# Weight fetches spread over the first pass: q and k in halves beside four batches, v and layer 2's weights behind the last batch

## The chip, the cores and the metric

The kernel runs on one core of a Trainium2 chip. A core has a matrix engine (TensorE, PE in the profile), three engines for elementwise work (VectorE or DVE, ScalarE or ACT, GpSimd or POOL) and a sequencer that here issues nearly all DMA transfers (SyncE, SP). Each engine works through its own list of instructions in order; semaphores hold an instruction until what it needs has been done. On-chip memory is SBUF (128 partitions) and PSUM (the matrix engine's accumulators). The metric is the device time of one execution in microseconds (us), the median of several runs.

## The reference, cut to what matters

The input x has 8 images of 512 channels and 32 x 32 = 1024 positions, in float32. Four layers follow each other; the change concerns the first two.

```
# layer 0: f, g, h are 64-channel products of x; f and g are batch-normalised over ALL 8 images
f = relu(batchnorm(Wf x));  g = relu(batchnorm(Wg x));  h = Wh x
attn = (f^T g) / largest_singular_value(f^T g)
x = Wv (attn applied to h) + x
# layer 1: group norm, then full attention over 1024 positions
n = groupnorm(x);  q = wq n + bq;  k = wk n + bk;  v = wv n + bv
x = x + wp (softmax(q^T k / sqrt(512)) applied to v) + bp
# layer 2: attention with 128 channels (W_w gives t, p, g; Z_w leads back), scaled, + x
# layer 3: sign(x + bias) times sign(W) with a scale, batch norm, + x, parametric relu
```

wq, wk, wv, wp and layer 3's W are 512 x 512, 1 MB each.

## The kernel before, in words

**The first pass.** Layer 0's batch norm needs the statistics of all 8 images before f and g can be used, so the kernel first reads every image once. The loop at line 1367 goes over the batches b = 0 to 7. `load_x` (line 136) fetches the 2 MB of a batch in four DMAs of 512 KB, one for each chunk of 128 channels (five for batch 0). The tile `xt` has two buffers, so the fetch of batch b waits until the matrix engine has read batch b-2 for the last time. For each batch the matrix engine makes f, g and (for b below 6) h, in 16 half-width matmuls per product, which the profile shows at line 1381; chunk by chunk for f, then for g, then for h. Two of them run side by side. Batches 6 and 7 stay in SBUF for the main part, which takes them first; the others are fetched again later.

**The weights of layer 1.** The scores need only wu = wq^T wk and the values only wo = wp wv, so the kernel multiplies the weights with each other first (`product`, line 1420). That needs q, k and v with the output channel on the partitions, while they lie in memory with the input channel there. `load_blocks` (line 1339) fetches such a matrix in 16 DMAs of 64 KB (q over four partition groups, r over four groups of rows; the issues carry line 1345), and `natural` (line 1350) turns it with four transposes of 32 x 32 blocks on VectorE (line 1355). Buffers are reused: turned q lies in w3's buffer, turned k in the buffer of q's blocks, turned v in that of k's blocks, and the matrix p (wp) later takes the buffer of v's blocks.

**Order of the fetches.** All of this goes through SP's single list, in the order of the loop: batch 1 and w3; batch 2 and all of q; batch 3 and all of k; batch 4, all of v and `load_rows` (11 small DMAs, lines 212 to 219); batch 5; batch 6 with z and tpg, the weights of layer 2 (line 156); batch 7; and p's four DMAs (line 1563), the first of them ahead of batch 7. The built program gives every DMA one of eight completion semaphores in turn, so each DMA issue also waits until the DMA eight places before it has landed.

**After the loop.** The matrix engine's order is written by hand from line 1581 on, with a generator `filler` (line 1556) that deals out work that depends on nothing urgent: the products for wu, the h of batches 6 and 7 (`late_h`), scaling of z, biases (`biases`, which reads turned k and p), Gram matrices, and last the products for wo (turned v times p). Between these pieces stands a chain of small steps, which normalises f and g (`relu`, line 1512), turns them (`turn`, line 1269), forms Gram matrices and finds the largest singular value by repeated squaring. The other engines' lists follow from the program's order and a scheduler that places each operation by its own estimate of when it can run.

**The main part** (from line 1645) then takes the 8 batches one after the other through all four layers; it is untouched.

Of the kernel before, what the change touches and what calls it, by code (L numbers as in the profile page):

```python
# [8 lines left out]
F32 = mybir.dt.float32  # L9
# [7 lines left out]
P = 128  # L17
# [53 lines left out]
QUAD = 32  # L71
GROUPS = 16
# [15 lines left out]
def kernel(  # L88
# [21 lines left out]
    wpool = ctx.enter_context(tc.tile_pool(name="weights", bufs=1))  # L110
# [8 lines left out]
    def wide():  # L119
        return psum["wide"].tile([P, N], F32, tag="wide", name="wide")  # L120
# [4 lines left out]
    def bank():  # L125
        return psum["bank"].tile([P, HF], F32, tag="bank", name="bank")
# [9 lines left out]
    def load_x(b, split=False):  # L136
        t = xpool.tile([P, CC, N], F32, tag="x", name="xt")
        src = x[b].rearrange("(cc p) n -> p cc n", p=P)
        for cc in range(CC):
            for ns in [half(h) for h in range(NH)] if split and not cc else [slice(0, N)]:  # L140
                nc.sync.dma_start(out=t[:, cc, ns], in_=src[:, cc, ns])
        return t

    def half(i):
        return bass.ts(i, HF)

    def side(i):

        return slice(i * MID, (i + 1) * MID)


    sbw = {}

    def load_w(name, src, shape, pool=wpool, eng=nc.sync, tag=None):
        t = pool.tile(shape, F32, tag=tag or name, name=name)
        eng.dma_start(out=t, in_=src)
        sbw[name] = t
        return t
# [4 lines left out]
    a1 = early.enter_context(tc.tile_pool(name="a1", bufs=1))  # L163
# [47 lines left out]
    def load_rows():  # L211
        nc.sync.dma_start(out=bg_row, in_=rows[MID + C :].partition_broadcast(P))
        rv = rows[MID : MID + C].rearrange("(q m b) -> q b m", q=4, b=QUAD)
        rq = cols.rearrange("(m b) n -> n b m", b=QUAD)
        for q in range(4):
            nc.sync.dma_start(out=bvc[bass.ts(q, QUAD), :], in_=rv[q])
            nc.sync.dma_start(out=bqc[bass.ts(q, QUAD), :], in_=rq[COL["L1_conv_bq"] + q])
        for i in range(2):
            nc.sync.dma_start(out=wv2[side(i), :], in_=w_v0)
# [58 lines left out]
    wu = wpool.tile([P, CC, C], F32, tag="wu", name="wu")  # L278
# [990 lines left out]
    def turn(b, src, dst, k):  # L1269

        tp = quad()
        for i in range(4):
            nc.tensor.transpose(tp[:, i, :], src[:, bass.ts(i, P)], ident)
        to = dst.rearrange("p (h t) c -> p h t c", t=4)[:, :, :, side(b % 2)]
        tp = tp.rearrange("p t (h c) -> p h t c", c=MID)
        if k:
            nc.scalar.copy(to, tp)
        else:
            nc.vector.tensor_copy(to, tp)

    def sign_weights():

        w3 = sbw["w3"]
        sign = a1.tile([P, CC, C], F16, tag="sign", name="sign")
        absw = a1.tile([P, 2, C], F32, tag="absw", name="absw")
        for cc in range(CC):
            nc.scalar.activation(sign[:, cc, :], w3[:, cc, :], AF.Sign)
            nc.scalar.activation(absw[:, min(cc, 1), :], w3[:, cc, :], AF.Abs)
            if cc:
                nc.vector.tensor_tensor(absw[:, 0, :], absw[:, 0, :], absw[:, 1, :], ALU.add)  # L1290
        lo, hi = sign[:, :, 0 : C // 2], sign[:, :, C // 2 :]
        nc.vector.scalar_tensor_tensor(sw3, hi, PACK, lo, ALU.mult, ALU.add)
        return absw[:, 0, :]
# [42 lines left out]

    nat = {}

    def load_blocks(name, src, tag):

        t = sbw[name] = a1.tile([P, 4, GROUPS, QUAD], F32, tag=tag, name="blocks_" + name)
        of = src.rearrange("(r a) c o -> r a c o", a=QUAD)
        for q in range(4):
            for r in range(4):
                nc.sync.dma_start(  # L1345
                    out=t[bass.ts(q, QUAD), r].rearrange("a (c m) b -> a c (m b)", c=CC),
                    in_=of[r][:, :, bass.ts(q, P)],
                )

    def natural(name, tag):  # L1350

        t = nat[name] = a1.tile([P, CC, C], F32, tag=tag, name="nat_" + name)
        to = t.rearrange("p o (c r a) -> p r c o a", r=4, a=QUAD)
        for r in range(4):
            nc.vector.transpose(to[:, r], sbw[name][:, r].rearrange("p (c o) b -> p c o b", o=CC))

    later = {
        1: [("w3", w_3, a1)],
        6: [("z", w_z, wpool), ("tpg", w_tpg, wpool)],
    }  # L1360
    shapes = {"z": [P, C], "tpg": [P, CC, 3 * P]}

# [4 lines left out]
    for b in range(B):  # L1367
        xt = load_x(b) if b else first
        for name, src, pool in later.get(b, ()):
            load_w(name, src, shapes.get(name, [P, CC, C]), pool)  # L1370
        if b in (2, 3, 4):
            load_blocks(*((("q", w_q, "q"), ("k", w_k, "k"), ("v", w_v, "v"))[b - 2]))
        if b == 4:
            load_rows()
        if b >= B - 2:
            resident[b] = xt
        banks = [bank() for _ in w0[: 3 if b < B - 2 else 2]]

        def products(i, cc):
            for h in range(NH):  # L1380
                mm(  # L1381
                    out=banks[i][side(h), :],
                    lhsT=w0[i][:, cc, :],
                    rhs=xt[:, cc, half(h)],
                    start=cc == 0,
                    stop=cc == CC - 1,
                )

        if b == 0:
            for cc in range(CC):  # L1390
                for i in range(2):
                    products(i, cc)
        for i in range(3):
            if i == 2 and b >= B - 2:
                continue
            if b or i == 2:
                for cc in range(CC):
                    products(i, cc)
            if i == 0:
                nc.scalar.copy(fs[b], banks[i])  # L1400
                nc.vector.bn_stats(st[:, 0, b, :], fs[b])
            elif i == 1:
                nc.vector.tensor_copy(gs[b], banks[i])
                nc.vector.bn_stats(st[:, 1, b, :], gs[b])
                if last is not None:
                    turn(last[0], last[1], ht_pair[last[0] // 2], 0)
        if b < B - 2:
            hraw = a2.tile([P, HF], F32, tag="hraw", name="hraw")
            nc.scalar.activation(hraw, banks[2], AF.Identity, bias=bhc)
            last = b, hraw  # L1410
        else:
            last = None
        if b == 3:
            total3 = sign_weights()
        if b == 5:
            scale_signs(total3)
        if b > 4:
            natural(*((("q", "w3"), ("k", "q"), ("v", "k"))[b - 5]))

    def product(lt, rhs, dst, vector):  # L1420
        for i in range(CC // 2):
            ps = wide()
            for k in range(2):
                for oc in range(CC):
                    one = mm(  # L1425
                        out=ps[:, half(k)],
                        lhsT=lt[:, oc, bass.ts(2 * i + k, P)],
                        rhs=rhs[:, oc, :],
                        start=oc == 0,
                        stop=oc == CC - 1,  # L1430
                    )
                    if i + k + oc == 0:
                        tc.keep_in_program_order(one)
                    if k == 0 or oc < CC - 1:
                        yield
            to = dst[:, 2 * i : 2 * i + 2, :].rearrange("p o c -> p (o c)")
            if i % 2 and vector:
                nc.vector.tensor_copy(to, ps)
            else:
                nc.scalar.copy(to, ps)  # L1440
            yield
# [114 lines left out]
    def filler():  # L1556

        t = sbw["p"] = a1.tile([P, CC, C], F32, tag="v", name="p")  # L1560
        of = w_p.rearrange("(m b) c o -> c b m o", b=QUAD)
        for q in range(4):
            nc.sync.dma_start(out=t[bass.ts(q, QUAD)], in_=of[q])
        yield from product(nat["q"], nat["k"], wu, True)
        for b in order[:2]:
            yield from late_h(b)
        yield from gram(jl, 2, ht_pair[jl], gtl)
        scale_z()
        yield
        between = biases()  # L1570
        sums = sums_u()
        for j in rest:
            for _ in grams(j):
                next(sums, None)
                yield
                if next(between, None):
                    yield
        yield from product(nat["v"], sbw["p"], wo, False)
# [251 lines left out]
```

## Time and profile before

| what | before |
|---|---|
| median of 3 runs (lowest to highest) | 1888.45 us (1888.18 to 1890.97) |
| time of the profiled execution | 1889.26 us |
| span in its profile, first to last instruction | 1887.4 us |
| matrix engine busy | 1855.8 us, 98% of the span |
| first pass, up to wu's first product | 0 to 103.83 us |
| hand-ordered stage after it, up to the main part's first product | 103.83 to 191.69 us |
| main part | 191.69 to 1887 us |
| DMA queue of SP: bytes over the span | 64.96 MB |

In the profile's lines a group is named by engine, line of the kernel, operation and tiles (out<-in); "x16" counts instructions; a bracket gives the idle time before the instruction and what ended it. PEld is the load of a matmul's stationary operand, which runs beside PE. SPq is SP's own time for issuing DMAs. PEclk is the clock that the matrix engine was granted, as a share of full speed.

### The profile page before, as it was taken

Reading aid. Unit: us, or ns where it says so; the run is one execution under the profiler, and the core shown is the slowest. Engines: PE = TensorE matmul, PEld = TensorE weight load, DVE = VectorE, ACT = ScalarE, POOL = GpSimd, SP = SyncE. Lnnn points to the kernel's source line nnn. Section 1 sums busy time; section 2 is a strip of 40 time slices with the busy share of each in tenths; the row PEclk is TensorE's granted clock in tenths of the full one; section 3 lists DMA queues with packets and bytes.
Section 4 is the critical chain, followed back from the end, with each engine's and each line's share of the span. In section 5 each row is a group of like instructions: output and inputs, shape, how many; then the busy total and the mean of one; then the engine's idle time right before and its main releaser. Section 6 shows DMA issues by size and latency. Waiting matters only on the chain.

```text
span 1887.4 us, 16534 instructions
## 1 busy us (share of the span) xinstructions
PE 1855.8 (98%) x6196; PEld 948.2 (50%) x6196; DVE 1121.6 (59%) x2083; ACT 542.0 (29%) x882; POOL 121.9 (6%) x109
## 2 busy tenths in 40 slices
PE   9799999999999999999999999999999999999997
PEld 4246455544645455544645455544645455544653
DVE  3246696467774666467764676357643766355447
ACT  2032221144203521244202522144202521244114
POOL 1000000100020000200020001100020001000011
PEclk9899999999999999999999999999999999999999
DMA  7720000002000110002000110001000200000001
GB/s 250 232 81 7 1 6 12 1 16 85 18 1 1 65 41 12 1 22 79 18 0 1 69 37 12 1 34 67 12 0 12 90 12 1 1 34 23 12 0 46
DMA packets 32738, 66.52 MB, mean 35 GB/s; under 512 B 4944, under 2 KB 12300, under 8 KB 32524
## 3 DMA queue, kind: packets, MB, share of 16 engines
q1 hardware_dynamic: 31724, 64.96, 10.3%
q8 instruction: 51, 0.84, 0.2%
q10 hardware_dynamic: 864, 0.43, 0.1%
q14 instruction: 35, 0.29, 0.0%
q0 software_dynamic: 64, 0.00, 0.0%
HBM read 46.44 MB, written 18.94 MB: 35 GB/s over the span
## 4 chain that ended last, share of the span: by engine, by line
PE 94%; DMA 2%; DVE 2%; SPq 1%; ACT 1%; issue 0%; POOL 0%; ACTq 0%; DVEq 0%
PE bank L412 46%; PE bank L590 20%; PE bank L992 6%; PE bank L839 6%; PE bank L691 3%; PE bank L708 3%; PE bank L1381 2%; DMA xt<-in_x 2%; PE bank L436 1%; PE bank L731 1%; PE wide L1425 1%; SPq L1345 1%; PE bank L1060 1%; PE bank L1483 1%; PE bank L862 0%
## 5 line engine op out<-in xcount | busy, mean ns | idle before, releaser
L590 PE MATMUL bank<-e,vt 128*128 128x512 f32 x768 | 336.2, 594 | 0.0
L590 PEld LDWEIGHTS bank<-e,vt 128*128 128x128 f32 x768 | 144.3, 190 | 172.3 <-issue 167.9
L412 PE MATMUL bank<-ut,h 128*128 128x512 f32 x384 | 178.9, 597 | 0.0
L412 PEld LDWEIGHTS bank<-ut,h 128*128 128x128 f32 x384 | 71.3, 190 | 94.7 <-issue 93.0
L412 PE MATMUL bank<-us,hs 128*128 128x512 f32 x256 | 115.6, 593 | 0.0
L839 PE MATMUL bank<-tpg 128*128 128x512 f32 x256 | 115.4, 595 | 0.0
L992 PE MATMUL bank<-e,tpg 128*128 128x512 f32 x256 | 114.7, 595 | 0.0
L363 DVE TENSOR_TENSOR e<-bank,e 128x512 f32<-128x512 f32 x96 | 66.1, 689 | 60.8 <-PE bank L412 42.4
L846 ACT ACTIVATE e<-bank 128x512 f32<-128x512 f32 x128 | 76.3, 597 | 67.0 <-PE bank L839 67.0
L412 PE MATMUL bank<-h,wu 128*128 128x512 f32 x192 | 89.0, 594 | 1.7 <-DVE h L487 1.7
L357 ACT COPY e<-bank 128x512 f32<-128x512 f32 x96 | 56.1, 585 | 118.9 <-PE bank L412 118.5
L412 PE MATMUL bank<-wo,h 128*128 128x256 f32 x384 | 89.9, 384 | 0.0
L243 POOL TENSOR_TENSOR r_r<-r_v,minus_half 128x4 f32<-128x4 f32 (+1 forms) x11 | 10.9, 989 | 1058.2 <-DVE r_v L242 1052.9
L1381 PE MATMUL bank<-xt,fg 128*64 128x512 f32 x256 | 63.7, 644 | 15.3 <-DMA xt<-in_x 10.7
L992 PEld LDWEIGHTS bank<-e,tpg 128*128 128x128 f32 x256 | 48.1, 190 | 60.4 <-issue 60.0
L412 PEld LDWEIGHTS bank<-wo,h 128*128 128x128 f32 x384 | 71.4, 190 | 12.6 <-issue 3.8
L412 PEld LDWEIGHTS bank<-us,hs 128*128 128x128 f32 x256 | 48.4, 190 | 57.5 <-issue 54.5
L851 DVE TENSOR_TENSOR esum<-esum,e 128x1024 f32<-128x1024 f32 x48 | 58.8, 1225 | 30.1 <-ACT e L846 29.9
L839 PEld LDWEIGHTS bank<-tpg 128*128 128x128 f32 x256 | 47.6, 190 | 55.0 <-issue 52.4
L719 ACT ACTIVATE sg<-xt,rb 128x512 f16<-128x512 f32 x64 | 44.2, 716 | 107.5 <-DVE xt L710 104.6
L363 DVE TENSOR_TENSOR vt<-bank,vt 128x512 f32<-128x512 f32 x48 | 33.2, 691 | 66.4 <-PE bank L412 65.6
L357 ACT COPY vt<-bank 128x512 f32<-128x512 f32 x64 | 37.3, 584 | 121.3 <-PE bank L412 121.2
(361 smaller groups left out, 2884.3 us busy)
## 6 DMA issues: line engine op xcount, KB each, us to landing
xt<-in_x SPq DMA_DIRECT2D x55, 512.0 KB
out<-both SPq DMA_DIRECT2D x63, 256.0 KB
rfull<-r_dram SPq DMA_DIRECT2D x15, 512.0 KB
f_dram<-f SPq DMA_DIRECT2D x8, 256.0 KB
fb<-f_dram SPq DMA_DIRECT2D x8, 256.0 KB
w<-in_w SPq DMA_DIRECT2D x1, 1024.0 KB
blocks_q<-in_w_q SPq DMA_DIRECT2D x16, 64.0 KB
blocks_k<-in_w_k SPq DMA_DIRECT2D x16, 64.0 KB
```

What stands on the lines that cost most here:

```text
L357: nc.scalar.copy(dst, ps)
L363: nc.vector.tensor_tensor(dst, ps, u, ALU.add)
L412: mm(out=ps[:, q * w : (q + 1) * w], lhsT=lt(ka, kb, q, k), rhs=rhs(ka, kb, q, k), start=first and q == 0 and k == 0, stop=last and k == 1 ...
L590: mm(out=ps, lhsT=a[:, t, bass.ts(r_, P)], rhs=e[t], start=first and t == 0, stop=last and t == NTH - 1, skip_group_check=True,)
L691: mm(out=ps[:, i, :], lhsT=xt[:, cc, bass.ts(4 * h + i, P)], rhs=sbw["tpg"][:, cc, 2 * P : 3 * P], start=cc == 0, stop=cc == CC - 1,)
L708: mm(out=ps, lhsT=sbw["z"][:, bass.ts(oc, P)], rhs=att, start=True, stop=True)
L719: nc.scalar.activation(sg[:, cc, :], xt[:, cc, half(h)], AF.Sign, bias=rb3[:, cc : cc + 1])
L839: mm(out=ps, lhsT=pt[:, 0, bass.ts(t, P)], rhs=tt[:, 0, half(h)], start=True, stop=True,)
L846: nc.scalar.activation(e[:, half(h)], ps, AF.Exp, scale=float(P) ** -0.5)
L851: nc.vector.tensor_tensor(esum, esum, e, ALU.add)
L992: mm(out=banks[h], lhsT=gt[:, t, :], rhs=es[t][:, half(h)], start=t == 0, stop=t == NT - 1,)
L1381: mm(out=banks[i][side(h), :], lhsT=w0[i][:, cc, :], rhs=xt[:, cc, half(h)], start=cc == 0, stop=cc == CC - 1,)
```

## The change

`load_blocks` takes the row groups r that it shall fetch, and keeps one tile per matrix over several calls. In the loop q's first half (r = 0, 1; 8 DMAs of 64 KB) is fetched beside batch 2, its second half beside batch 3, k's halves beside batches 4 and 5. z and tpg move from batch 6 to batch 7, and v's 16 DMAs come behind the loop. `natural` runs for q at b = 6 and for k at b = 7 (one batch later than before), and for v in `filler`, behind wu's products and ahead of the h of batches 6 and 7. The fetch of p moves behind it, for it reuses the buffer of v's blocks. No operation is added or removed, no shape or buffer changes.

```diff
-    def load_blocks(name, src, tag):
-        t = sbw[name] = a1.tile([P, 4, GROUPS, QUAD], F32, tag=tag, name="blocks_" + name)
+    def load_blocks(name, src, parts):
+        if name not in sbw:
+            sbw[name] = a1.tile([P, 4, GROUPS, QUAD], F32, tag=name, name="blocks_" + name)
+        t = sbw[name]
         of = src.rearrange("(r a) c o -> r a c o", a=QUAD)
         for q in range(4):
-            for r in range(4):
+            for r in parts:
                 nc.sync.dma_start(
...
     later = {
         1: [("w3", w_3, a1)],
-        6: [("z", w_z, wpool), ("tpg", w_tpg, wpool)],
+        7: [("z", w_z, wpool), ("tpg", w_tpg, wpool)],
     }
...
-        if b in (2, 3, 4):
-            load_blocks(*((("q", w_q, "q"), ("k", w_k, "k"), ("v", w_v, "v"))[b - 2]))
+        if b in (2, 3, 4, 5):
+            load_blocks(*((("q", w_q), ("k", w_k))[b // 2 - 1]), ((0, 1), (2, 3))[b % 2])
         if b == 4:
             load_rows()
...
-        if b > 4:
-            natural(*((("q", "w3"), ("k", "q"), ("v", "k"))[b - 5]))
+        if b > 5:
+            natural(*((("q", "w3"), ("k", "q"))[b - 6]))
+    load_blocks("v", w_v, range(4))
...
     def filler():
+        yield from product(nat["q"], nat["k"], wu, True)
+        natural("v", "k")
         t = sbw["p"] = a1.tile([P, CC, C], F32, tag="v", name="p")
         of = w_p.rearrange("(m b) c o -> c b m o", b=QUAD)
         for q in range(4):
             nc.sync.dma_start(out=t[bass.ts(q, QUAD)], in_=of[q])
-        yield from product(nat["q"], nat["k"], wu, True)
         for b in order[:2]:
             yield from late_h(b)
```

## The prediction, made before the changed kernel had run

> **What bounds the kernel now.** I read the page's slices first (40 slices of 47 us), then the windows of the three stages, since an average of 98% hides where the matrix engine stands still.
>
> ```profile
> PE   9799999999999999999999999999999999999997
> PEclk9899999999999999999999999999999999999999
> DMA  7720000002000110002000110001000200000001
> ...
> 0.00:103.83 103.83, 88.56 (x385) 34.27 (x385) 32.69 (x79) 14.47 (x23) 5.09 (x26) 0.95 0.73 230
> 103.83:191.69 87.86, 82.27 (x706) 50.34 (x705) 49.95 (x166) 30.88 (x60) 2.27 (x3) 1.00 0.10 34
> ```
>
> In the window lines the columns are length, busy PE, PEld, DVE, ACT, POOL, then granted clock, DMA share, GB/s. Only the first pass (to 103.83 us) is both short of matrix work (88.56 of 103.83 busy), slowed in clock (0.95), and full of DMA (0.73). Everything later is bound by the matrix engine with DMA nearly idle, and its order is relative: nothing there happens at a fixed time. So what the first pass gains or loses should appear in the end.
>
> Next the matrix engine's timeline around the hole, in microseconds from the start and duration:
>
> ```profile
> 38.93 7.09 PE L1381 MATMUL bank<-xt,fg 128*64 128x512 f32 x32
> 46.53 3.65 PE L1381 MATMUL bank<-xt,h 128*64 128x512 f32 x16
> 51.84 1.08 PE L1381 MATMUL bank<-xt,fg 128*64 128x512 f32 x4 [1.66 <-DMA xt<-in_x]
> 53.29 1.08 PE L1381 MATMUL bank<-xt,fg 128*64 128x512 f32 x4 [0.37 <-DMA xt<-in_x]
> 55.12 1.08 PE L1381 MATMUL bank<-xt,fg 128*64 128x512 f32 x4 [0.75 <-DMA xt<-in_x]
> 58.15 6.21 PE L1381 MATMUL bank<-xt,fg 128*64 128x512 f32 x20 [1.95 <-DMA xt<-in_x]
> 64.88 3.65 PE L1381 MATMUL bank<-xt,h 128*64 128x512 f32 x16
> 74.55 5.71 PE L1381 MATMUL bank<-xt,fg 128*64 128x512 f32 x14 [6.02 <-DMA xt<-in_x]
> ```
>
> Batch 3 runs without a hole; batches 4 and 5 wait for their x chunk by chunk, and run slowly behind each wait: in the window 74.5 to 84.1 the clock was 0.73. The size of the loss, from starts: batch 2 starts at 27.89 and batch 3 at 38.93, so a batch with h takes 11.04 us. From batch 3's start to the end of batch 7 (38.93 to 103.9) lie 65.0 us; unstalled they would be 3 x 11.04 (batches 3, 4, 5) + 1.0 (the eight small L1298 matmuls, 88.22 to 89.21) + 7.6 (batch 6, 89.21 to 96.81) + 7.09 (batch 7) = 48.8. The loss is **16.2 us**.
>
> Then why x is late, from the chain of waits between 40 and 76 us:
>
> ```profile
> 33.98 7.88 DMA xt<-in_x
> 41.88 0.56 SPq L1345
> ...
> 46.97 0.60 SPq L1345
> ...
> 47.67 0.53 SPq L141
> ...
> 49.37 8.73 DMA xt<-in_x
> 58.12 0.56 SPq L1345
> ...
> 69.70 0.60 SPq L219
> 70.39 4.02 DMA xt<-in_x
> ```
>
> SP issues in order, and a DMA waits for the one eight places before it. So of 16 blocks seven go out at once, the eighth waits until x has landed (41.88, 58.12), and it and eight more follow at 0.64 us each. Only then does SP reach the next batch's x, at 47.67 and, with 6.0 us of row loads besides, at 70.39. The buffer of xt had been free since about 39 and 50. SP's issue time bounds this, not bandwidth: between 41.9 and 47.6 the blocks move 9 x 64 KB in 5.7 us, about 100 GB/s, where x moved at about 410 GB/s after 76 us.
>
> **What the Trainium skill says.** "DMA: Bandwidth & Descriptors", Rules for kernel authors, says that transfers of less than 64 KB are mostly overhead; these, at the edge, agree with it: 0.64 us of SP each. The same page, Anatomy of one DMA: a semaphore wait is made by the issuing sequencer before dispatch, the DMA engines never wait. That is the stall above: one waiting block holds back all x behind it. "TensorE: Matmul & The Clock Gate", Part 1: after about 3.4 us idle the clock is halved until a busy window of like length; the trace agrees in kind, with 6.21 us for 20 matmuls after 58.15 (20/32 of 7.09 is 4.43). The same page, Architectural detail: VectorE's queue is strictly first in, first out. That matters for v.
>
> **The change part by part.**
>
> *The halves.* With 8 blocks beside batch 2 the eighth still waits for x2 at 26.66, but is then the last: SP is free at 27.3 instead of 32.4. Batch 3's x waits for its buffer (batch 1 ends at 24.41 + 3.65 = 28.06), goes out at 28.1 and, since in before it landed 9.4 us after its first issue beside seven blocks (32.47 to 41.88), lands at 37.5; the matrix engine wants it at 38.93. Batch 4: SP free at 38.1, buffer at 35.45 + 3.65 = 39.1, landed 9.4 to 10.4 us later (47.67 to 58.12 is the other example), at 48.5 to 49.5; wanted at 49.97. Both stalls are gone.
>
> *Batch 5.* Half of k's blocks and the row loads stand before it. Eighth block at 48.5 to 49.5, + 0.6, + 6.0 for the rows: x5 goes out at 55.1 to 56.1. Its chunks arrive, as batch 4's did in before (51.84, 53.29, 55.12, 58.15 against 47.67), 4.2, 5.6, 7.4 and 10.4 us later; without blocks beside them the last came after about 8.5 (a load at 78.84 against 70.39). Last chunk: 63.6 to 66.5. The matrix engine starts batch 5 at 61.0 and wants the last chunk 2.65 later, at 63.7. So 0 to 2.8 us of stall remain, and 0 to 1.8 of slow clock behind it (6.21 against 4.43 above). I take **2.5** of loss.
>
> *Batches 6 and 7.* The eighth block of k's second half waits for x5 (65.1), so x6 goes out at about 65.7 and lands 8.5 later, at 74.2; wanted at 61.0 + 11.04 + 1.0 + 2.5 = 75.6. Batch 7 goes out when batch 5 is read, about 74.6, first chunk 78.8; wanted at 83.2. No stall. Batch 7 ends at about 90.3 instead of 103.9.
>
> *z, tpg and v last.* They leave SP's path ahead of x and stand behind x7: 2 MB of x, 1 MB of z and tpg, and seven blocks at about 400 GB/s are 8.6 us, with start-up about 12, so tpg lands at 86.6; nine blocks at 0.64 follow, last issue 92.4, landed about 2.5 later (estimate from traffic of the last v block, 63.75 to about 65.9): **95**. The built order puts v's four transposes on VectorE between the turn copies ft and gt (at 113.6 in before, which is 9.7 us after batch 7's end) and the Gram copies. At 90.3 + 9.7 = 100 they find v landed, 5 us early. They cost 4 x 0.62 = 2.47 us (the row at 66.21), and VectorE stands idle there:
>
> ```profile
> 113.82 0.69 DVE L1279 COPY gt<-quad 128x512 f32<-128x512 f32 x1 [0.18 <-PE quad L1273]
> 116.76 0.22 DVE L1492 COPY gm<-bank 64x64 f32<-64x64 f32 x1 [2.25 <-PE bank L1483]
> 118.91 0.22 DVE L1492 COPY gg_full<-bank 64x64 f32<-64x64 f32 x1 [1.93 <-PE bank L1483]
> ```
>
> One transpose (0.62) stands ahead of gt in a gap of 0.18, so gt is 0.4 late; but the gt Gram waits for ScalarE's gt copy, which ends at 116.0, later anyway. Two fit into 2.25, one into 1.93. Cost 0; bound 2.5 if that cover is gone.
>
> *The rest at nothing.* q's and k's transposes fall on idle VectorE too (k's second half is due at about 69, landed at about 68 to 70, with the copy of g at batch 6 the next on the queue, some 10 us later). f's write-out behind v's blocks on SP: ready at about 98, SP free at 93. p now waits for v's transposes, goes out at about 104 and needs some 7 us; biases and wo use it from about 42 us after batch 7 (146 in before), 132. fb of batch 7 comes behind p; batch 7 enters only in the main part. Cover of tens of microseconds in each.
>
> *Sum.* 16.2 - 2.5 - 0 to 0.5 for v = 13.5 us. Profiled execution 1889.26 (1.9 over the span, 0.8 over the median) - 13.5 = 1875.8; against the median, **1875.0 us**.
>
> **The rivals.** (a) Batch 5's x comes in time: 16.2 gained, 1872.2. For it: 63.6 is the early end of its arrival; against it: seven blocks run beside it, and all x beside blocks took 9.4 to 10.4. (b) SP still starves the pass: x4 or x5 or x6 later than I think, each followed by a slow clock (batch 5 lost 6.02 + about 2.5 in before). Half of the gain goes: 8 us left, 1880.5. For it: the margin of batch 4 is 0.5 to 1.5 us on its first chunk and that of x6 1.4. (c) Slower: v is late for VectorE. The first transpose heads a strict queue, behind it stand gt and the Gram copies, and behind those the singular value chain and then the matrix engine. Every microsecond past 100 costs one; the kernel is slower only if v lands after 100 + 13.5 = 113.5, 18 us later than worked out; at 120 it would be 1895. Against it: tpg and 16 blocks would need twice their time. (d) No change: the next stage is bound by ScalarE's activations, say, so gains are given back. Against it: that stage starts from batch 7's last product, and all in it moves along. 1888.5.
>
> **How the numbers follow.** Likeliest, 12 to 15 us gained (1873.5 to 1876.5): 0.50. Rival (a), over 15: 0.22. Rival (b), between 4 and 12: 0.20. (d), within 0.2% (3.8 us, about what a measurement here can tell from no change): 0.04. (c) or another slowdown: 0.04. Faster is thus 0.92. The range runs from 16.9 gained (all stalls and a little of the first batches') to 7.5 gained, 1871.5 to 1881.0, which leaves out the tails of (b), (c) and (d).
>
> **What would show it.** In the profile after: no wait for xt at batches 3, 4, 6 and 7, up to 2.8 us at batch 5; batch 7 ending near 90; clock near 1 in that window; wu's products starting there; v's transposes running at about 100 without a wait for a DMA; the hand-ordered stage still 88 us, the main part 1695. I am wrong if VectorE waits for v's blocks, if SP reaches x5 much after 56, or if the stage after the pass grows by what the pass lost.

## The result, and the profile after

The changed kernel takes 1875.08 us in the median (1874.54 to 1875.96), beside 1888.62 us for the kernel before on the same chip: a ratio of 0.9926, with a 95% interval of 0.9909 to 0.9943. It is faster by 13.5 us. Two later comparisons of the same two kernels gave 0.9924 (0.9910 to 0.9937) and 0.9931 (0.9917 to 0.9944). The forecast was 1875.0 us. The profiled execution took 1875.41 us (1889.26 before), its span is 1873.6 us (1887.4).

The page's slices of the changed kernel, and its three stages as windows (length, busy PE, PEld, DVE, ACT, POOL, granted clock, DMA share, GB/s):

```profile
PE   9999999999999999999999999999999999999997
PEclk9999999999999999999999999999999999999999
DMA  8620000002000200002000200001000200000001
...
0.00:89.88 89.88, 83.46 (x384) 33.83 (x384) 30.36 (x75) 14.49 (x23) 5.09 (x26) 1.00 0.76 249
89.88:177.66 87.78, 82.28 (x707) 50.34 (x705) 52.21 (x170) 30.90 (x60) 2.27 (x3) 1.00 0.17 51
177.66:1873.00 1695.34, 1685.03 (x5108) 863.56 (x5108) 1039.09 (x1839) 496.98 (x799) 114.53 (x80) 1.00 0.07 23
```

The whole gain is in the first row: 103.83 us have become 89.88, and the clock of that stage 1.00 instead of 0.95. The second stage is as long as before (87.78 for 87.86) although VectorE does 2.3 us more there (v's transposes), and the main part is unchanged. Nothing was given back.

The matrix engine's timeline, batches 3 to 7 of the changed kernel:

```profile
38.50 7.04 PE L1383 MATMUL bank<-xt,fg 128*64 128x512 f32 x32
...
49.54 7.04 PE L1383 MATMUL bank<-xt,fg 128*64 128x512 f32 x32
...
60.58 1.89 PE L1383 MATMUL bank<-xt,fg 128*64 128x512 f32 x8
63.30 1.08 PE L1383 MATMUL bank<-xt,fg 128*64 128x512 f32 x4 [0.84 <-DMA xt<-in_x]
65.62 4.51 PE L1383 MATMUL bank<-xt,fg 128*64 128x512 f32 x20 [1.23 <-DMA xt<-in_x]
...
82.86 7.09 PE L1383 MATMUL bank<-xt,fg 128*64 128x512 f32 x32
89.88 2.84 PE L1428 MATMUL wide<-nat_k,nat_q 128*128 128x512 f32 x6
```

Batches 3, 4, 6 and 7 follow without a wait. Only batch 5 still waits, 2.1 us in two pieces; behind them 20 matmuls take 4.51 us, full speed, where they took 6.21 behind batch 4's waits in before. The chain of waits names what stood ahead of batch 5's x:

```profile
40.04 6.87 DMA xt<-in_x
46.92 0.56 SPq L1347
47.53 1.31 SPq L212
...
53.25 0.60 SPq L219
...
55.47 10.10 DMA xt<-in_x
65.62 4.51 PE bank L1383 x20
```

One block (line 1347) after batch 4's landing, then 6.4 us of row loads, then x. Nine blocks per batch had stood there before.

### The profile page after: what moved, and what is told of

Its sections match the earlier page's. It is cut to its first block, busy times and chain, and to the rows that moved or that the text cites. A ratio compares the mean times of both kernels' runs of the same rounds, so it can differ in the third digit from the quotient of the medians.

```text
span 1873.6 us, 16533 instructions
## 1 busy us (share of the span) xinstructions
PE 1850.8 (99%) x6196; PEld 947.7 (51%) x6196; DVE 1121.7 (60%) x2083; ACT 542.4 (29%) x882; POOL 121.9 (7%) x109
## 4 chain that ended last, share of the span: by engine, by line
PE 95%; DVE 2%; DMA 1%; ACT 1%; SPq 0%; issue 0%; POOL 0%; ACTq 0%; DVEq 0%
PE bank L412 46%; PE bank L590 21%; PE bank L992 6%; PE bank L839 6%; PE bank L691 3%; PE bank L708 3%; PE bank L1383 3%; PE bank L731 1%; PE bank L436 1%; DMA xt<-in_x 1%; PE wide L1428 1%; PE bank L1060 1%; PE bank L1486 1%; PE bank L862 0%; PE quad L1273 0%; DVE st L448 0%
## 5 line engine op out<-in xcount | busy, mean ns | idle before, releaser
L412 PEld LDWEIGHTS bank<-wo,h 128*128 128x128 f32 x384 | 71.4, 190 | 12.6 <-issue 3.8
L363 DVE TENSOR_TENSOR vt<-bank,vt 128x512 f32<-128x512 f32 x48 | 33.2, 691 | 66.4 <-PE bank L412 65.6
L357 ACT COPY ut<-bank 128x512 f32<-128x512 f32 x48 | 28.1, 586 | 128.7 <-PE bank L412 128.7
```

The costliest lines, as they stand in the source:

```text
L357: nc.scalar.copy(dst, ps)
L363: nc.vector.tensor_tensor(dst, ps, u, ALU.add)
L412: mm(out=ps[:, q * w : (q + 1) * w], lhsT=lt(ka, kb, q, k), rhs=rhs(ka, kb, q, k), start=first and q == 0 and k == 0, stop=last and k == 1 ...
```

## The experiments

Three measures help to compare them, all read from the matrix engine's timeline of one profiled execution. "First pass" runs from the first matmul to wu's first product; it leaves out the start, which varies by 0.6 us between profiles. "Batches 0, 1" runs from the first matmul to batch 2's first. "Lost at" a batch is what lies over 11.04 us between the h products of the batch before and its own; 11.04 is the spacing without a wait. All are in us.

| kernel | first pass | batches 0, 1 | lost at 4 | lost at 5 | hand-ordered stage | time, median |
|---|---|---|---|---|---|---|
| before | 99.30 | 23.4 | 7.3 | 8.7 | 87.86 | 1888.6 |
| changed | 85.53 | 23.1 | 0 | 2.5 | 87.78 | 1875.1 |
| changed, again | 83.54 | 23.6 | 0 | 0 | 87.76 | 1873.8 |
| changed, third time | 84.17 | 23.6 | 0 | 0.6 | 87.77 | 1874.4 |
| v alone last | 86.94 | 24.3 | 2.5 | 0.2 | 88.30 | 1876.8 |
| halves alone | 95.20 | 23.4 | 0 | 11.9 | 87.93 | 1885.2 |
| rows behind v | 83.28 | 23.3 | 0 | 0 | 87.77 | 1873.0 |
| k's second half at 6 | 83.44 | 23.5 | 0 | 0.1 | 87.76 | 1873.3 |
| both of these | 83.24 | 23.3 | 0 | 0.1 | 87.75 | 1873.4 |
| z, tpg at 6 | 88.94 | 24.2 | 0 | 4.8 | 87.76 | 1874.8 |
| blocks by GpSimd, free | 94.29 | 27.2 | 0 | 0 | 87.87 | 1884.4 |
| blocks by GpSimd, held back | 87.89 | 23.4 | 4.6 | 0 | 89.36 | 1880.6 |
| v fetched four times | 84.79 | 23.5 | 0 | 1.4 | 98.45 | 1885.0 |

Four profiles have no wait for x at all and take 83.24 to 83.54 us; what separates them lies mostly in batches 0 and 1, which took 23.1 to 24.3 us wherever the edit did not reach them. The floor is taken as 83.2 to 83.3, so before lost 16.0 us against it (16.2 was worked out). The kernel before took 1888.0 to 1888.6 us beside them, and the ratios ran from 0.9919 to 0.9986; those of the kernels within 1 us of the changed one have overlapping intervals.

**Which part brings it: v alone.** In the kernel before, v's fetch goes behind the loop, its transposes into the filler, p behind them; q and k stay whole.

```diff
-        if b in (2, 3, 4):
-            load_blocks(*((("q", w_q, "q"), ("k", w_k, "k"), ("v", w_v, "v"))[b - 2]))
+        if b in (2, 3):
+            load_blocks(*((("q", w_q, "q"), ("k", w_k, "k"))[b - 2]))
...
-        if b > 4:
-            natural(*((("q", "w3"), ("k", "q"), ("v", "k"))[b - 5]))
+        if b in (5, 6):
+            natural(*((("q", "w3"), ("k", "q"))[b - 5]))
+    load_blocks("v", w_v, "v")
...
```

> The kernel before with one part of the change alone: v fetched behind the loop, turned in the filler, p behind it; q and k whole beside batches 2 and 3. Theory (16 blocks beside batch 3 still hold batch 4's x, but nothing more than the row loads holds batch 5's): batch 4 loses 3.5 us of waiting and up to 1.8 of slow clock, batch 5 nothing; 11 to 12.7 of the 16.2 us are gained, batch 7 ends between 91 and 93, 1876.8 us. Rival (the halves are what counts, v last only takes 1 MB off): 3 to 5 us gained, 1884.

Measured: 1876.81 us, ratio 0.9939 (0.9922 to 0.9955). The pass is 3.7 us over the floor: 2.5 at batch 4, 0.2 at batch 5, and 1.0 in batches 0 and 1, which the edit does not touch. Batch 4:

```profile
47.30 3.65 PE L1381 MATMUL bank<-xt,h 128*64 128x512 f32 x16
51.37 1.08 PE L1381 MATMUL bank<-xt,fg 128*64 128x512 f32 x4 [0.41 <-DMA xt<-in_x]
52.61 1.08 PE L1381 MATMUL bank<-xt,fg 128*64 128x512 f32 x4 [0.16 <-DMA xt<-in_x]
54.27 1.08 PE L1381 MATMUL bank<-xt,fg 128*64 128x512 f32 x4 [0.59 <-DMA xt<-in_x]
55.83 4.51 PE L1381 MATMUL bank<-xt,fg 128*64 128x512 f32 x20 [0.48 <-DMA xt<-in_x]
```

Batch 4's x went out at 47.05, still behind 16 blocks of k; batch 5 no longer waits. This one part gives 12 of the 16 us.

More than batch 5's loss went: batch 4 lost 7.3 us in before and 2.5 here, though the same 16 blocks stand ahead of its x. Three things differ. Seven blocks of v no longer run beside it, and its last chunk came 8.7 us after it went out instead of 10.5. It went out 3.7 us ahead of the time at which batch 4 wanted it, instead of 2.3, mostly because batches 0 and 1 ran late in this profile. And behind its shorter waits 20 matmuls took 4.51 us, full speed, instead of 6.21. So what runs beside x has a price as well as what stands ahead of it.

**The halves alone.** In the changed kernel v is fetched whole beside batch 4 again.

```diff
         if b == 4:
+            load_blocks("v", w_v, range(4))
             load_rows()
...
-    load_blocks("v", w_v, range(4))
```

> The changed kernel with v whole beside batch 4, as before: the halves alone. Theory (SP's list order): 24 blocks and the row loads stand ahead of batch 5's x, 17 of the blocks at 0.64 us behind batch 4's landing (46.9), so it goes out near 64 us, arrives from 68 to 74; batch 5 loses 10.8 us and 1.8 of slow clock, batches 3, 4, 6, 7 nothing; 3.7 us gained, 1885. Rival (each part brings its share): 8 us gained, 1880.5.

Measured: 1885.22 us, ratio 0.9986 (0.9979 to 0.9993); 11.9 us over the floor.

```profile
57.34 3.65 PE L1384 MATMUL bank<-xt,h 128*64 128x512 f32 x16
69.73 10.01 PE L1384 MATMUL bank<-xt,fg 128*64 128x512 f32 x32 [8.74 <-DMA xt<-in_x]
80.26 3.65 PE L1384 MATMUL bank<-xt,h 128*64 128x512 f32 x16
```

The halves take batch 4's wait away and leave batch 5 one wait of 8.74 us, which costs 3.0 us more in slow clock (10.01 for 7.04). Batch 5's buffer was free at 49.95, with batch 3's last product, but its x went out only at 65.06, behind the blocks and row loads. In that time the DMA engines were far from busy (share 0.35, 102 GB/s at the end of the line):

```profile
50.00:60.00 10.00, 10.00 (x50) 3.38 (x48) 3.79 (x6) 1.27 (x2) 0.00 (x0) 1.00 0.35 102
```

So it is SP's list that holds this x, not the engines' bandwidth. The rival expectation, 8 us from the halves, fell: they bring 4.1 of the pass and v alone 12.4, together 16.5, about what the whole change brings (13.8 to 15.8 in its three profiles). But they are not one batch each: v alone cures batch 5 and most of batch 4, the halves cure batch 4 and leave batch 5 worse than in before (11.9 lost instead of 8.7).

**What is left at batch 5.** Two ways to clear it: the row loads behind v, or k's second half beside batch 6.

```diff
-        if b == 4:
-            load_rows()
...
     load_blocks("v", w_v, range(4))
+    load_rows()
```

> The changed kernel with the 11 row loads (6.4 us of SP) behind v instead of ahead of batch 5. Theory (SP's list order decides when x goes out): batch 5's x goes out when its buffer is free, about 49.6 us instead of 53.95, and even if it again lands 11.7 us later, that is 61.3, before the 63.2 at which it is wanted; the stall of 2.1 us and the rest of batch 5's 2.5 us loss go, batch 7 ends near 87.5, time 2.5 us under the changed kernel, 1872.6. Rival (the 2.5 us are the floor of DMA bandwidth in this pass): no change, 1875.

```diff
-        if b in (2, 3, 4, 5):
-            load_blocks(*((("q", w_q), ("k", w_k))[b // 2 - 1]), ((0, 1), (2, 3))[b % 2])
+        if b in (2, 3, 4, 6):
+            load_blocks(*((("q", w_q), ("k", w_k))[b // 4]), ((0, 1), (2, 3))[b in (3, 6)])
```

> The changed kernel with k's second half fetched beside batch 6 instead of 5. Theory (blocks running beside x slow its last chunks): batch 5's x still goes out at about 54 us, but lands 8.5 us later as x did without blocks, at 62.4, before 63.2; stall gone, 1872.8. Rival (the 6.4 us of row loads alone make it late, blocks beside it cost x nothing): x lands near 65.6 again, 1875. k is turned later, but 15 us ahead of wu's first product.

The unaltered changed kernel as the measure beside these two, then once more as the measure beside both edits together:

> The changed kernel unaltered, as the measure for the runs beside it: 1875 us, batch 5 waiting about 2 us for its x, batch 7 ending near 90 us.

> The changed kernel unaltered once more, as the measure beside the next: 1874 to 1875 us; in its profile batch 5 waits between 0 and 2.6 us for its x, as in the two profiles so far.

> The changed kernel with both the row loads behind v and k's second half beside batch 6. Theory (either of them takes batch 5's wait away, and without waits the pass is bound by the matrix engine): nothing beyond what each gave alone, 1872.5 to 1873.5 us, batch 7 ending 83.1 us after the first matmul. Rival (some x is still late in part of the executions): 1 us less than either, 1871.8.

Measured: in all three versions (rows, k's half, both) the wait is gone, the pass is 83.24 to 83.44 us. But the unaltered kernel beside them had hardly a wait either:

```profile
50.37 7.04 PE L1383 MATMUL bank<-xt,fg 128*64 128x512 f32 x32
57.93 3.65 PE L1383 MATMUL bank<-xt,h 128*64 128x512 f32 x16
61.41 7.04 PE L1383 MATMUL bank<-xt,fg 128*64 128x512 f32 x32
```

Batch 5 here starts at 61.41 and runs through, in the same program that waited 2.1 us above; the third profile waited 0.43. So the 2.5 us that both theories expected to win back are there in some executions only. The gain measured was 0.8 us for the rows (1872.98 beside 1873.80), 0.5 for k's half (1873.28 beside 1873.80) and 1.1 for both (1873.38 beside 1874.44). The intervals of the ratios overlap; only for both together did the highest time (1873.72) lie below the lowest of the changed kernel (1873.83). These are the fastest versions found, by a margin of 1 us that is hardly more than the measurement can tell. The expectation of 2.5 was wrong in size: it took one profile's wait for the usual one.

**z and tpg.** Back beside batch 6:

```diff
-        7: [("z", w_z, wpool), ("tpg", w_tpg, wpool)],
+        6: [("z", w_z, wpool), ("tpg", w_tpg, wpool)],
```

> The changed kernel with z and tpg fetched behind batch 6 again, as in before. Theory (batch 7's x waits for its buffer at about 74 us anyway, z and tpg run in that gap): no change, 1875, within 0.5 us in the end of batch 7. Rival (their 1 MB stands ahead of batch 7's x and delays it): up to 2.5 us more, 1877.5.

Measured: 1874.79 us (1873.64 to 1878.35) beside 1873.80. Its profile fell on the longest execution, with a long wait at batch 5, which comes before the edit has any part in it (SP issues the same DMAs in the same order up to then, and z at 70.07):

```profile
64.00 1.08 PE L1383 MATMUL bank<-xt,fg 128*64 128x512 f32 x4 [0.54 <-DMA xt<-in_x]
67.12 6.17 PE L1383 MATMUL bank<-xt,fg 128*64 128x512 f32 x20 [2.04 <-DMA xt<-in_x]
...
78.37 7.14 PE L1383 MATMUL bank<-xt,fg 128*64 128x512 f32 x32
86.03 7.14 PE L1383 MATMUL bank<-xt,fg 128*64 128x512 f32 x32
```

Batches 6 and 7 run without a wait with z and tpg in their old place, as the theory had it; moving them brings nothing that these runs show. Batch 5 lost 4.8 us (6.17 us for 20 matmuls is slow clock again) and batches 0 and 1 another 0.9. The 1 us in the median can't be given to the edit, for batch 5 varies by more. Still, two of these five executions took over 1877 us and none of the changed kernel's fourteen over 1876; that the edit has no part in this is argued from SP's list, not shown.

**SP's list or the DMA engines?** If only SP's list held x, another queue for the blocks should free it. In the kernel before:

```diff
-                nc.sync.dma_start(
+                nc.gpsimd.dma_start(
                     out=t[bass.ts(q, QUAD), r].rearrange("a (c m) b -> a c (m b)", c=CC),
```

> The kernel before with the 48 block fetches issued by GpSimd's queue, which is idle in the pass; bytes and pieces are the same. Theory (it is SP's list, not the DMA engines' bandwidth, that holds x): x goes out as its buffers come free, batch 7 ends between 87.5 and 91, 1873 to 1876 us. Rival (the DMA engines are the limit: small pieces cost the same from any queue): more than half of the 16.2 us stays, 1881 or more.

Measured: 1884.35 us, ratio 0.9977 (0.9968 to 0.9986). The theory's number failed: 11 us over the floor, now 3.9 in batches 0 and 1 and 7.2 at batch 2, for GpSimd with nothing else to do had issued all three matrices by 45.5 us. The window from 10 to 45 us:

```profile
10.00:45.00 35.00, 29.20 (x121) 9.00 (x117) 12.18 (x27) 7.29 (x13) 21.36 (x40) 0.90 1.00 278
```

The DMA engines were busy all the time (share 1.00) at 278 GB/s, where they moved about 410 without blocks (in before, from 76 us on). So their time counts too. The pieces are not the same, other than the expectation has it: the profile counts 6912 packets for the 48 blocks on SP's queue and 1536 on GpSimd's. The rate of busy engines is alike, though: in before, from 50.0 to 58.1 us, with SP's blocks beside x, the share was 1.01 at 281 GB/s.

To take the early crowding away, each matrix is held until its batch's x has begun to land; q and k are turned one batch later and v in the filler, as in the changed kernel:

```diff
+        nc.gpsimd.tensor_copy(t[:, :, 0, 0:1], xt[:, 0, 0:4].unsqueeze(2))
...
-                nc.sync.dma_start(
+                nc.gpsimd.dma_start(
                     out=t[bass.ts(q, QUAD), r].rearrange("a (c m) b -> a c (m b)", c=CC),
```

> The kernel before with q, k and v whole beside batches 2, 3 and 4 as they were, but issued by GpSimd's queue, each matrix held back by a small GpSimd copy until the first chunk of that batch's x has landed (the run with the free GpSimd queue fetched all three in the first 45 us and so crowded batches 0 to 2); v is turned in the filler and p fetched behind it, as in the changed kernel. Theory (SP's list holds x, and is all): x goes out as buffers come free, batches 3 to 7 wait 3 us at most in sum, batch 7 ends between 88 and 93, 1873 to 1878 us. Rival (the DMA engines' own time counts too: with blocks beside x they were busy throughout at 240 to 295 GB/s, and a batch with 1 MB of blocks needs 3.1 MB in 11.04 us, 285 GB/s): several batches wait, with slow clock behind, batch 7 ends between 94 and 98, 1879 to 1884 us.

Measured: 1880.57 us, ratio 0.9961 (0.9948 to 0.9975). The pass is 87.89 us, 4.6 over the floor; q, k and v stand whole beside batches 2, 3 and 4 as in before, and 11.4 of the 16 us are gone. Batch 4 alone waits:

```profile
49.75 1.89 PE L1386 MATMUL bank<-xt,fg 128*64 128x512 f32 x8
52.81 1.08 PE L1386 MATMUL bank<-xt,fg 128*64 128x512 f32 x4 [1.18 <-DMA xt<-in_x]
55.42 5.96 PE L1386 MATMUL bank<-xt,fg 128*64 128x512 f32 x20 [1.52 <-DMA xt<-in_x]
```

Its x went out at 38.97, when its buffer was free, and its last chunk was there at 55.4; from 30 to 60 us the engines' share was 1.04 at 288 GB/s, busy without a break. (One of its four DMAs waited until 40.45 for a row load that had gone out at 29.70; even the row loads were slow.) So with the blocks out of SP's list some 11 us of the loss go; the 4.6 us that stay fall where the DMA engines are busy. (The split is not quite clean: the build also placed the row loads, z and tpg earlier in this kernel's SP list, between batches 2 and 4, and a block took about 7 us from issue to landing on GpSimd's queue. What SP's own queue would do to x with the list out of the way is not shown.) The pass ended at 92.1, inside the theory's 88 to 93, but the time missed its 1873 to 1878: the stage behind it is 1.6 us longer. There v's transposes, held in program order, run in one piece at 116.2 and stand in the chain of waits; the matrix engine's next wait behind them is 1.77 us, where the changed kernel has 0.20.

```profile
116.29 2.40 DVE nat_v L1356 x4
```

**A late v.** Rival (c) of the prediction: in the changed kernel v is fetched four times into the same buffer, and its transposes are held in program order.

```diff
-    load_blocks("v", w_v, range(4))
+    for _ in range(4):
+        load_blocks("v", w_v, range(4))
```

> The changed kernel with v fetched four times over into the same buffer, so that it lands some 31 us later, near 126 instead of 95 us. The build places v's transposes later for that, among the operations at about 144 us. Theory (a late v costs through what is queued behind it): VectorE does not wait, but p, which takes v's buffer, goes out only near 145, lands near 151, and the second set of bias products waits for it, about 7 us: 1882. Rival (v and p have slack for all of it): no change, 1875.

Measured: 1885.03 us, ratio 0.9984 (0.9974 to 0.9993), 10 us over the changed kernel; the pass is not touched, the stage after it grows from 87.78 to 98.45. SP's v fetches ended at 123.7. The matrix engine's wait, then VectorE's, from the two timelines:

```profile
154.95 1.83 PE L1469 MATMUL bank<-ones,part 128*128 128x1 f32 x8 [8.06 <-DVE part L1462]
```

```profile
141.31 1.29 DVE L1357 STREAM_TRANSPOSE nat_v<-blocks_v 128x512 f32<-128x512 f32 x2
142.63 0.68 DVE L1357 STREAM_TRANSPOSE nat_v<-blocks_v 128x512 f32<-128x512 f32 x1
...
151.95 0.49 DVE L1460 TENSOR_SCALAR part<-p,bvc 128x512 f32<-128x512 f32 x1 [4.16 <-DMA p<-in_w_p]
```

VectorE never waits for v, because the build set v's transposes at 141, 17.6 us after v's last DMA had gone out. What is late is p, which takes v's buffer, went out at 144.07 and kept the bias products 8.06 us. The expectation was 7. The other 2.5 us come behind that wait in slow clock: the same transposes of f by the matrix engine take 1.04 us before it and 1.95 after it (granted clock 0.50 from 154.9 to 161.0 us), and from these bias products to wo's first product it is 9.4 us instead of the changed kernel's 6.9.

```profile
137.27 1.04 PE L1273 MATMUL quad<-ident,f 128*128 128x128 f32 x8
156.65 1.95 PE L1273 MATMUL quad<-ident,f 128*128 128x128 f32 x8
```

So a late v cost through p. Whether it can also hold VectorE's queue, as rival (c) told it, is not shown: VectorE had been given the transposes so late that v was never what it waited for. How much of that placing comes from v's late arrival and how much from holding the transposes in program order is not separated; held, but with v early, they ran at 116.2 in the run above.

## Why the prediction was right

*The size of the hole.* 16.2 us of loss in the first pass, from starts of batches: against the floor of the profiles without a wait it is 16.0. Right.

*Its cause.* The blocked block in SP's list. For batch 5, 8.7 of the 16.0 us, this is shown. In before its x went out at 70.39, its buffer free since 50.2, and from 60 to 70 us, while it stood in the list, the DMA engines were little used (share 0.27, 61 GB/s):

```profile
60.00:70.00 10.00, 8.53 (x36) 2.55 (x32) 4.87 (x8) 0.69 (x1) 0.00 (x0) 0.87 0.27 61
```

With more blocks in that place batch 5 lost 11.9 (12.6 expected), with none 0.2. For batch 4's 7.3 us, "SP's issue time bounds this, not bandwidth" was too strong: its x went out late through the list, but once out it shared busy engines with seven blocks (share 1.01 from 50.0 to 58.1 us), and with v's blocks gone and the list ahead of it as long as before it lost 2.5 (3.5 and up to 1.8 of slow clock expected). The runs with GpSimd's queue say the same: with the list out of the way, 4.6 us of loss stay while the DMA engines are busy. The step rested on blocks moving 100 GB/s when nothing ran beside them, and didn't ask what they take from x when they do. The forecast didn't suffer, since its arrival times were taken from loads with blocks beside them, and the change takes blocks out of both: v leaves the crowded stretch, q and k are thinned to half a batch each.

*Batches 3 and 4.* Expected without a wait; so they are. x of batch 3 went out at 27.68 (28.1 expected), that of batch 4 at 38.71 (39.1) and landed at 46.91 (48.5 to 49.5 expected). The margin was larger than rival (b) has it: the landing times that it compares with batch 4's first product are those of the last chunk, which is wanted 2.65 us later. Measured, all of x was there 2.6 us ahead of the first product.

*Batch 5.* Went out at 53.95 (55.1 to 56.1 expected), its last chunk came at 65.6 (63.6 to 66.5): earlier out, 11.7 us on the way instead of 8.5 to 10.4. Loss at batch 5 2.5 us, 2.5 predicted. That agreement is partly luck: in two other profiles of the same program the loss was 0 and 0.6, with v fetched four times 1.4, and with z and tpg moved 4.8, neither of which should matter yet. Rival (a), "batch 5's x comes in time", is what happens in part of the executions. In the four of these profiles that waited, x was 9.7 to 11.7 us on the way. More load doesn't explain it: over that time the engines moved 2.8 MB at a share of 0.81 in the profile that lost 2.5 us, and 2.7 MB at a share of 1.00 in the one without a wait, where x took about 8.5 us. Why x lands sooner in one execution than in another is not settled here; the margin is near zero, so small differences decide.

*z, tpg and v last.* The working has a small slip: its 2 MB, 1 MB and seven blocks are 3.6 million bytes, 9.0 us at 400 GB/s, not 8.6; 5 us of margin cover it. SP's last v issue ended at 93.04 (92.4 predicted), and VectorE, which comes there at 99.6, finds v landed:

```profile
99.00 0.69 DVE L1279 COPY ft<-quad 128x512 f32<-128x512 f32 x1 [2.52 <-PE quad L1273]
99.61 0.70 DVE L1357 STREAM_TRANSPOSE nat_v<-blocks_v 128x512 f32<-128x512 f32 x1
100.23 0.65 DVE L1279 COPY gt<-quad 128x512 f32<-128x512 f32 x1
100.81 1.29 DVE L1357 STREAM_TRANSPOSE nat_v<-blocks_v 128x512 f32<-128x512 f32 x2
102.82 0.22 DVE L1495 COPY gm<-bank 64x64 f32<-64x64 f32 x1 [0.73 <-PE bank L1486]
102.96 0.69 DVE L1357 STREAM_TRANSPOSE nat_v<-blocks_v 128x512 f32<-128x512 f32 x1
104.97 0.22 DVE L1495 COPY gg_full<-bank 64x64 f32<-64x64 f32 x1 [1.31 <-PE bank L1486]
```

No transpose waits for a DMA, and VectorE still idles 0.73 and 1.31 us ahead of the Gram copies: the cover held, cost 0. Out of that cover, in the run with GpSimd's fetches held back, the stage was 1.6 us longer, under the 2.5 that was given as the bound.

*The sum.* Pass 13.8 us shorter, the other stages within 0.3: 13.5 predicted, 13.5 measured in the medians (14.5 and 13.6 in the two later comparisons). The mechanism was right in the main; that the sum fits to 0.1 us is luck at batch 5. Rival (d) fell, as the stage behind the pass moved along whole. Rival (b) did not come in the profiled run, but the 4.8 us above is of its kind.

## What to carry to other kernels

A queue that issues in order turns one waiting transfer into a wait of everything behind it: count, for each transfer that the bound engine needs next, what stands ahead of it in the list, and move what is needed late behind what is needed soon. Look at the DMA share while the transfer waits: low, and the list holds it; near 1, and the bytes beside it count too. Check then that the moved transfer's followers (here p, which takes its buffer) still come in time. And where a wait's margin is near zero, look at several profiles before pricing its removal.

## What the runs showed of the hardware that was not expected

- With blocks of 64 KB beside x the DMA engines were fully busy at 278 to 288 GB/s in all on GpSimd's queue and at 281 on SP's, against about 410 without blocks. On GpSimd's queue such a block took 7.4 us from issue to landing (k's), and SP's row loads up to 10.7 us in that crowd.
- The same program had waits of 0, 0.43 and 2.1 us at the same place in three profiles.
- Slow clock follows waiting in no simple proportion. Waits of 2.1 us in 5 left full speed (4.51 us for 20 matmuls), 2.6 and 2.7 us in 5 to 6 cost 1.5 to 1.7 us (6.17 and 5.96), and one wait of 8.74 us cost 3.0. The Trainium skill ("TensorE: Matmul & The Clock Gate", Part 1) says that the clock is judged over windows of about 3.4 us that run free of the program. The uneven cost is compatible with that, though no run here varied the phase. The prediction took from the same place that about 3.4 us of idle time halve the clock. Less was enough here: ahead of the 6.17 us no single wait was longer than 2.04 us, ahead of the 5.96 none longer than 1.52.
